# A four-layer graph network on one core: the set-up of its sparse path is laid out anew, in one order for all engines

## The chip, the core and the metric

The kernel runs on one core of a Trainium2 chip. The core has five engines with instruction streams of their own: TensorE (PE in the profile, with its weight loads as PEld), VectorE (DVE), ScalarE (ACT), GpSimd (POOL) and SyncE (SP). SP, ACT and POOL also issue transfers, and an issue stands in the same queue as the engine's other instructions. The metric is the device time of one execution in microseconds (us); lower is better.

## The reference

There are 128 graphs of 64 nodes with 128 features, and one weighted adjacency matrix for each. About a quarter of its entries are not zero, and their values reach just under 6. Four layers follow one another, each `x = layernorm(x + layer(x, adj))`:

```python
# layers 0 and 1: a filter network on every pair (i, j), then a weighted sum over j
f   = exp(coeff * (d_ij - offsets)**2)            # 20 or 64 values for a pair
W   = softplus-like(f @ w1 + b1) @ w2 + b2
agg = einsum('bjf,bijf->bif', y, W * weight_ij)   # layer 0: cosine cutoff at 5; layer 1: adj squared
out = softplus-like(agg @ o1 + c1) @ o2 + c2
# layers 2 and 3: graph convolutions with a normalised adjacency
out = einsum('bij,bjh->bih', norm_A, h @ W) + b
```

The filter network is the bulk of the work. Entries that are zero have a weight of zero in layer 1 and one common filter value in layer 0, so only entries that are not zero need it.

## The kernel before, in words

`sparse_stack` takes two graphs together as a pair (64 pairs, `NP`), eight pairs as a set (`NS` = 8 sets). The nodes of a graph are ranked by how many entries lie below the cutoff (`close`), and the rows of the adjacency are permuted by rank, so that rows of like length can share a fixed number of slots (`CAPS`). For each set `nearest` finds the entries of each row with VectorE's max8 and find-index, and `pack` writes distances (`d`), column numbers (`j`) and weights (`w`) of the slots to DRAM. The main loop has three chunks for each pair and layer (index `i`, `n, k = divmod(i, 3)`): `filter_in` (matmul `px`, exponential), `gather` (matmul `pg` with a one-hot `hot`), `softplus`, `filter_out` (matmul `pw`), `message` (VectorE `m`) and `slot_sums`. At `k` = 0 the loop issues pair n + 2's `d` loads, at `k` = 1 its `j` and `w` loads; `gaussians(n + 1, k)` squares and exponentiates the next pair's `d` on ACT. Searches of later sets run inside the loop, a few steps at a time, from the generator `gathering()`.

Ahead of the loop stands the set-up:

- Four loads of the adjacency (`entries`, L886), two masks on each quarter (L887 and L888), two counts by halving (`count`, L812 to L815). `close` is the difference of these.
- A key for each graph, so that graphs can be sorted by size: `keys`, `place_on`, `to` (L898 to L910). `indirect_dma_start` then scatters the adjacency to `adj_sorted` (2 MB), and later x to `x_sorted` (4 MB, staged in unused parts of `x_all` and `a_all`).
- `rank(0, ...)` (L820 to L842) gives the rank of each node; `rank(1, ...)`, on the degree, is for layer 1.
- `permuted(0)`: set 0 is permuted by matmuls with one-hots (`there`, L1059 and L1060), copied out of PSUM (`rows`), stored to DRAM (`perm`, L1066) and read back in another layout (`ad`, L1071). Later sets are permuted by scatters of POOL, read back at L1052.
- `goes_to(0)` (L980 to L992) makes the places of all pairs in the sorted order, `find_rows` (L997 to L1005) the rows for the output's scatter.
- A small chain gives the filter of a zero entry: `g0`, two activations, `zero_x`, two activations, `zero_w` (L1464 to L1474), and at L1481 VectorE's `zero_filter`.
- `compact(0)` runs `nearest(0)` and `pack(0, 0)`; `loads(0)` and `loads(1)` (L1299) read the slots of the first two pairs, `permuted(1)` and `load_x(1)` (L1331) ready set 1, and two transfers lay out `caps` (L1880, L1881).

The order in an engine's stream is made by a scheduling pass of the framework, unless `in_order` chains instructions to the order in which the program states them:

```python
    before_loop = block[-1]
    in_order(first, before_loop, (nc.vector, nc.gpsimd))
    ...
    in_order(before_loop, block[-1], (nc.tensor, nc.scalar, nc.vector, nc.gpsimd, nc.sync))
```

So in the set-up VectorE and GpSimd are each chained, while the pass is free with PE, ACT and SP, and it may move what stands in the loop ahead of it: in the trace rank 1's pieces lie between those of `nearest(0)`.

Of the kernel before, what the change touches and what calls it, by code (L numbers as in the profile page):

```python
# [12 lines left out]
F32 = mybir.dt.float32  # L13
# [6 lines left out]
P = 128  # L20
# [581 lines left out]
def sparse_stack(ctx: ExitStack, tc: tile.TileContext, t: dict, out: bass.AP, flag):  # L602
# [122 lines left out]

    def load_matrix(name, rows=C):
        w = const.tile([rows, C], F32, name=f"w_{name}")
        nc.scalar.dma_start(w, t[name])
        return w
# [4 lines left out]
    def load_column(name):  # L734
        b = const.tile([P, 1], F32, name=f"c_{name}")
        nc.scalar.dma_start(b, column(name))
        return b
# [19 lines left out]
    def load_rows(name):  # L757
        b = const.tile([P, C], F32, name=f"b_{name}")
        nc.scalar.dma_start(b, dram_ap(t[name], 0, [[0, P], [1, C]]))
        return b  # L760
# [18 lines left out]


# [96 lines left out]
    with (  # L877
        tc.tile_pool(name="count", bufs=2) as pre,
        tc.tile_pool(name="count_ps", bufs=1, space=PSUM) as ps_pre,
    ):  # L880
        entries = pre.tile([NB, A, A], F32, name="entries", bufs=1)
        some = pre.tile([NB, A, A], BF16, name="some", bufs=1)
        within = pre.tile([NB, A, A], BF16, name="within", bufs=1)
        for q in range(4):
            cut = slice(16 * q, 16 * (q + 1))
            nc.sync.dma_start(entries[:, cut, :], adj[:, cut, :])  # L886
            nc.vector.tensor_scalar(within[:, cut, :], entries[:, cut, :], CUTOFF, None, ALU.is_lt)  # L887
            nc.vector.tensor_scalar(some[:, cut, :], entries[:, cut, :], 0.0, None, ALU.is_gt)  # L888

        for into, at in x_parts:  # L890
            nc.sync.dma_start(into, x_flat[:, at])

        degree, close = given[:, 0, :], given[:, 1, :]
        run(deque([count(some, pre, degree), count(within, pre, close)]), -1)
        nc.vector.scalar_tensor_tensor(close, close, -float(A), degree, ALU.add, ALU.add)

        total = const.tile([NB, 1], F32, name="total")
        nc.vector.tensor_reduce(total, given[:, 0:2, :], AX.XY, ALU.add)  # L898
        nc.vector.tensor_scalar(total, total, key_of[:, 0:1], key_of[:, 1:2], ALU.mult, ALU.add)
        keys = pre.tile([P, P], F32, name="keys", bufs=1)  # L900
        nc.vector.tensor_scalar(keys, ident, total, None, ALU.mult)
        keys_ps = ps_pre.tile([P, P], F32, name="keys_ps")
        nc.tensor.matmul(keys_ps, lhsT=all_ones, rhs=keys, start=True, stop=True)
        ranking = deque([rank(0, close, pre)])
        run(ranking, 16)
        nc.vector.tensor_scalar(keys, keys_ps, total, None, ALU.is_gt)
        nc.vector.tensor_reduce(total, keys, AX.X, ALU.add)
        nc.vector.tensor_scalar(place_on, columns, total, None, ALU.is_equal)
        to = const.tile([NB, 1], U32, name="graph_to")
        nc.vector.tensor_copy(to, total)  # L910
        nc.gpsimd.indirect_dma_start(
            out=adj_sorted.rearrange("g i j -> g (i j)"),
            out_offset=bass.IndirectOffsetOnAxis(ap=to, axis=0),
            in_=entries.rearrange("g i j -> g (i j)"), in_offset=None,
        )
        run(ranking, -1)
        nc.vector.tensor_mul(width0, width0, width0)
        nc.vector.reciprocal(coeff0, width0)
        nc.vector.tensor_scalar(coeff0, coeff0, -0.5, None, ALU.mult)
        nc.vector.tensor_scalar(neg_off[0], neg_off[0], -1.0, None, ALU.mult)  # L920

        below = pre.tile([NB, A * A], BF16, name="below", bufs=1)
        nc.scalar.activation(
            below, entries.rearrange("g i j -> g (i j)"), AF.Relu, scale=-1.0, accum_out=odd[:, 0:1]
        )

    work = ctx.enter_context(tc.tile_pool(name="swork", bufs=2))
    node = ctx.enter_context(tc.tile_pool(name="snode", bufs=2))
    ps_x = ctx.enter_context(tc.tile_pool(name="sps_x", bufs=1, space=PSUM))
    ps_g = ctx.enter_context(tc.tile_pool(name="sps_g", bufs=1, space=PSUM))  # L930
    ps_w = ctx.enter_context(tc.tile_pool(name="sps_w", bufs=1, space=PSUM))


    compacting = ctx.enter_context(ExitStack())
    cpt = compacting.enter_context(tc.tile_pool(name="scompact", bufs=1))
# [18 lines left out]


# [15 lines left out]

    def goes_to(i):
        if i == 0:
            sorted_ = ps_n.tile([P, 512], F32, tag="n", name="sorted")[:, 0 : 3 * A]
            nc.tensor.matmul(
                sorted_, lhsT=place_on, rhs=given.rearrange("g k i -> g (k i)"),
                start=True, stop=True,
            )
        from_ = sorted_[:, 2 * A :] if i == 0 else places[1]
        nc.vector.tensor_scalar(codes[i], from_, row[:, 2:3], None, ALU.add)  # L980
        tp = ps_n.tile([P, 512], F32, tag="n", name=f"goes_t{i}")
        nc.tensor.transpose(tp[0:A, 0:P], rows_on if i else codes[0], ident)
        by_pair = tp[0:A, 0:P].rearrange("i (p b) -> i p b", b=2)
        for b in range(2):
            to = slice(b * A, (b + 1) * A)
            nc.vector.tensor_copy(a_all[to, :, A] if i else index[to, :], by_pair[:, :, b])

        code = const.tile([P, A], BF16, name=f"code_b{i}")
        nc.vector.tensor_copy(code, codes[i])
        nc.sync.dma_start(code_dram[i], code)  # L990
        if i == 0:
            nc.vector.tensor_copy(table.rearrange("g k i -> g (k i)"), sorted_[:, 0 : 2 * A])  # L992

    def find_rows():

        tp = ps_n.tile([P, 512], F32, tag="n", name="graphs")
        nc.tensor.matmul(tp[:, 0:P], lhsT=row_wide, rhs=place_on, start=True, stop=True)  # L997
        by_pair = tp[:, 0:P].rearrange("i (p b) -> i p b", b=2)
        row_f = spare[:, 5 * P : 5 * P + NP]
        for b in range(2):  # L1000
            half_ = slice(b * A, (b + 1) * A)
            nc.vector.tensor_scalar(
                row_f[half_], by_pair[half_, :, b], float(A), near[half_], ALU.mult, ALU.add
            )
        nc.vector.tensor_copy(at_row, row_f)  # L1005


# [27 lines left out]
    def permuted(s, again=False):  # L1035
# [18 lines left out]
        if s == 0 and not again:  # L1054
            goes_first()
            flat = ps_x.tile([P, 2, 512], F32, tag="x", name="permuted0")[:, 0, :]
# [11 lines left out]
            )  # L1068
            for h, engine in enumerate((nc.sync, nc.scalar)):
                from_ = perm0.rearrange("k (q h r) j -> h (k q) r j", h=2, r=8)[h]  # L1070
                engine.dma_start(ad[64 * h : 64 * (h + 1), :, 0:A], from_)  # L1071
        permuted_rows[s] = ad
        yield

    def goes_on(s):

# [958 lines left out]
```

## Time and profile before

| | |
|---|---|
| median of 3 runs | 1592.23 us (1591.06 to 1595.87) |
| the profiled execution | 1607.39 us, span 1605.5 us |
| mean granted TensorE clock in it | 0.982 |
| busy in the span | PE 1432.6 us (89%), DVE 1355.6 (84%), ACT 1335.6 (83%), POOL 732.5 (46%) |
| first filter matmul starts | 75.25 us |
| first and fourth message start | 84.89 us and 100.64 us |

A row of the timeline gives the start and the duration in us, the engine, the line of the kernel, the operation, the tile written and those read, how many in a row were merged, and in brackets how long the engine sat idle before it and what ended that. ACTq, SPq and POOLq are issues of transfers; their duration is the issue, not the transfer. A row of waits gives the sum, the times and the longest. A row of a DMA queue gives packets, MB and the share of the 16 engines' time: q0 carries GpSimd's scatters, q1 SP's transfers, q10 ACT's.

### The profile page before, as it was taken

The page shows a single profiled execution, that of the slowest core. Times are in us where ns is not written, and L with a number is a line of the kernel's source. Part 1 is how long each engine was busy: PE and PEld are TensorE (multiplying, and loading weights), DVE is VectorE, ACT ScalarE, POOL GpSimd, SP SyncE. Part 2 cuts the span into 40 slices and gives each one's busy share as a digit, 9 for nine tenths or more (in the row PEclk, how much of TensorE's full clock was granted, in tenths as well). Part 3 has the DMA queues.
Part 4 walks back from the last instruction along what each step waited for, and adds up shares of the span by engine and source line. Part 5 has one row for each costly group of instructions (what it writes and reads, how often), then busy time and mean ns, then how long its engine had stood idle before and what let it go on. Part 6 is the DMA issues. An engine that isn't in the chain of part 4 may idle for free.

```text
span 1605.5 us, 24221 instructions
## 1 busy us (share of the span) xinstructions
PE 1432.6 (89%) x6813; PEld 802.6 (50%) x6813; DVE 1355.6 (84%) x3547; ACT 1335.6 (83%) x1847; POOL 732.5 (46%) x1174
## 2 busy tenths in 40 slices
PE   1276999999999999999999999999999999999974
PEld 1133454555554555555445555556555555555543
DVE  7687889999989999889878888888888888888873
ACT  1266898989888989889999998999989999899842
POOL 2425246555655644425611255433554435543454
PEclk9998999999999999999999999999999999999976
DMA  7654464645455544447555455544554455455200
GB/s 257 209 123 114 112 138 123 135 124 145 124 136 134 136 122 113 113 111 178 149 151 129 128 142 132 129 124 125 144 132 120 120 134 138 124 141 123 64 8 23
DMA packets 122289, 205.67 MB, mean 128 GB/s; under 512 B 47956, under 2 KB 80034, under 8 KB 121506
## 3 DMA queue, kind: packets, MB, share of 16 engines
q1 hardware_dynamic: 110784, 187.61, 46.7%
q0 software_dynamic: 6576, 14.99, 2.9%
q10 hardware_dynamic: 4786, 1.43, 0.4%
q8 instruction: 57, 0.93, 0.3%
q14 instruction: 86, 0.70, 0.2%
HBM read 185.29 MB, written 18.64 MB: 127 GB/s over the span
## 4 chain that ended last, share of the span: by engine, by line
PE 45%; DVE 27%; ACT 10%; DMA 7%; issue 6%; SPq 3%; POOL 2%; another core or an unknown queue 1%; ACTq 0%; DVEq 0%; POOLq 0%
PE pw L1788 16%; PE px L1774 9%; DVE m L1814 8%; PE pg L1800 7%; DVE agg L1837 6%; ACT h L951 4%; DVE hot L1762 2%; DVE at L1182 2%; PE hw L1673 2%; SPq L1299 2%; ACT g L951 2%; PE y L1453 2%; ACT d L951 1%; DVE st L1415 1%; PE o L1584 1%
## 5 line engine op out<-in xcount | busy, mean ns | idle before, releaser
L951 ACT ACTIVATE h<-h,half 128x672 f32<-128x672 f32 (+13 forms) x385 | 353.1, 917 | 0.1
L1837 DVE TENSOR_REDUCE agg<-m 128x16 f32<-128x240 f32 (+13 forms) x896 | 325.0, 411 | 3.0
L951 ACT ACTIVATE g<-pg 128x672 f32<-128x672 f32 (+12 forms) x384 | 303.2, 790 | 26.4 <-DVE m L1814 13.2
L1800 PE MATMUL pg<-hot,ys 64*128 64x336 f32 (+12 forms) x1536 | 308.8, 478 | 7.9 <-DVE hot L1762 7.0
L1788 PE MATMUL pw<-h,w_L_gnn_W2T 128*128 128x420 f32 (+5 forms) x768 | 301.9, 516 | 15.2 <-DVE m L1814 15.2
L1814 DVE SCALAR_TENSOR_TENSOR m<-pw,c_L_gnn_b,g 128x840 f32<-128x840 f32 (+5 forms) x192 | 200.9, 1046 | 115.6 <-PE pw L1788 88.0
L1788 PE MATMUL pw<-h,w_L_gnn_fw 128*128 128x336 f32 (+6 forms) x768 | 264.4, 467 | 28.3 <-DVE m L1814 22.0
L951 ACT ACTIVATE h<-px,c_L_gnn_b 128x840 f32<-128x840 f32 (+5 forms) x192 | 178.7, 931 | 53.6 <-PE px L1774 52.8
L1814 DVE SCALAR_TENSOR_TENSOR m<-pw,c_L_gnn_fb,g 128x672 f32<-128x672 f32 (+6 forms) x192 | 176.9, 921 | 50.0 <-PE pw L1788 31.2
L951 ACT ACTIVATE h<-px,c_L_gnn_fb 128x672 f32<-128x672 f32 (+6 forms) x192 | 159.3, 830 | 71.2 <-PE px L1774 46.4
L1788 PEld LDWEIGHTS pw<-h,w_L_gnn_W2T 128*128 128x128 f32 x768 | 132.5, 191 | 141.1 <-DVE m L1814 37.6
L1774 PE MATMUL px<-d,fw 64*128 64x336 f32 (+6 forms) x768 | 166.2, 507 | 40.8 <-DMA d<-d_dram 29.2
L1800 PEld LDWEIGHTS pg<-hot,ys 64*128 64x128 f32 x1536 | 146.3, 188 | 108.1 <-issue 17.5
L1788 PEld LDWEIGHTS pw<-h,w_L_gnn_fw 128*128 128x128 f32 x768 | 132.5, 191 | 120.6 <-DVE m L1814 62.2
L1762 DVE SCALAR_TENSOR_TENSOR hot<-j,row,w 128x1212 f32<-128x1212 bf16 (+12 forms) x128 | 177.0, 1383 | 9.0 <-issue 9.0
L1774 PE MATMUL px<-d,w1t 64*128 64x420 f32 (+5 forms) x768 | 181.1, 548 | 1.7 <-ACT h L951 1.6
L1422 POOL TENSOR_SCALAR rs<-mv 128x4 f32<-128x4 f32 x61 | 14.5, 237 | 344.0 <-DVE mv L1416 335.6
L1774 PEld LDWEIGHTS px<-d,fw 64*128 64x128 f32 x768 | 59.7, 188 | 132.2 <-ACT h L951 44.4
L951 ACT ACTIVATE d<-d,neg_off 128x1212 f32<-128x1212 f32 (+12 forms) x128 | 119.8, 936 | 7.1 <-issue 7.1
L1428 POOL TENSOR_SCALAR x_all<-ny,mv,rs 128x128 f32<-128x128 f32 x124 | 116.4, 947 | 3.3
L1030 POOL DMA_INDIRECT rows<-comb,goes x64 | 67.9, 1061 | 97.1 <-DMA rows<-comb,goes 69.6
L1774 PEld LDWEIGHTS px<-d,w1t 64*128 64x128 f32 x768 | 57.8, 184 | 66.8 <-ACT g L951 26.8
(264 smaller groups left out, 2209.6 us busy)
## 6 DMA issues: line engine op xcount, KB each, us to landing
d<-d_dram SPq DMA_DIRECT2D x32, 315.0 KB
w<-w_dram SPq DMA_DIRECT2D x32, 315.0 KB
d<-d_dram SPq DMA_DIRECT2D x32, 303.0 KB
w<-w_dram SPq DMA_DIRECT2D x32, 303.0 KB
w<-w_dram SPq DMA_DIRECT2D x32, 252.0 KB
j<-j_dram SPq DMA_DIRECT2D x32, 157.5 KB
j<-j_dram SPq DMA_DIRECT2D x32, 151.5 KB
d<-d_dram SPq DMA_DIRECT2D x16, 300.0 KB
```

Source lines behind the costliest of these rows:

```text
L951: latest = nc.scalar.activation(out_, in_, func, **kw)
L1030: nc.gpsimd.indirect_dma_start(out=into, out_offset=bass.IndirectOffsetOnAxis(ap=at, axis=0), in_=rows, in_offset=None,)
L1182: nc.vector.max_index(out=at[:, r, cut], in_max=top[:, r, cut], in_values=av[:, r, :])
L1299: (engine if name == "d" else nc.sync).dma_start(to, dram_ap(slots[layer, name][s], first, [[0, to.shape[0]], [1, n]]))
L1428: (nc.gpsimd if n == GS else nc.vector).tensor_scalar(dst[:, s, :], y[:, s, :], mv[:, s, 0:1], rstd[:, s : s + 1], ALU.subtract, ALU.mult,)
L1453: nc.tensor.matmul(ps[:, s, :], lhsT=xt[:, s * P : (s + 1) * P], rhs=w["win"], start=True, stop=True)
L1762: nc.vector.scalar_tensor_tensor(hots[n][:, 0:size], j[:, 0:size], near, wt[:, 0:size], ALU.is_equal, ALU.mult)
L1774: nc.tensor.matmul(ps[:, b, 0:n], lhsT=w1, rhs=d[rows, col : col + n], start=True, stop=True)
L1788: nc.tensor.matmul(c["pw"][:, b, :], lhsT=c["w"]["w2"], rhs=c["h"][:, b, :], start=True, stop=True)
L1800: nc.tensor.matmul(ps[:, b, 0:n], lhsT=y[rows, :], rhs=hots[c["n"]][rows, at], start=True, stop=True,)
L1814: nc.vector.scalar_tensor_tensor(messages[n][:, :, at], c["pw"], c["w"]["b2"], c["g"], ALU.add, ALU.mult)
L1837: nc.vector.tensor_reduce(av[:, :, :, r], both, AX.X, ALU.add)
```

## The change

The set-up is stated in a new order, and one chain holds all five engines to it from the start of the set-up to the end of the kernel.

- Layer 0's constants are loaded first, on ACT's queue; those of layer 1 and of the convolutions follow behind the first permutation, on SP's queue.
- The two masks are combined into `within`, so that `close` comes from one count; `rank(0)` follows at once, and `permuted(0)` up to the store of `perm`. The mask `some`, the count `degree`, the graph keys and the scatters of the adjacency and of x stand behind that; the loads of `ad` are stated after the scatters. Set 0's own loads (`load_a(0)` and x) are stated ahead of the loads of the staged x.
- `below` is computed by `act`, which loads ACT's table; the permuted rows use a bank of `ps_n`.
- `goes_to(0)` and two `load_a` follow the later constants; `find_rows` moves to just ahead of the loop. `zero_filter` is stated ahead of the search.
- In `pack(0, 0)` the sine is stated ahead of the store of `j`, the square of `w` is GpSimd's, and the loads of the first two pairs are stated right after the store of `w`. Four of pair 0's six `d` loads are on ACT's queue, the others on SP's.
- `rank(1)` runs to its first halving after those loads and ends after the first one-hot, before the loop; `gathering()` waits 31 steps in its place.

```diff
+    queue = [nc.scalar]            # load_matrix, load_column and load_rows use queue[0]
...
+    layers = [filter_layer(0)]
+    queue[0] = nc.sync
...
+        for cut in quarters:
+            nc.sync.dma_start(entries[:, cut, :], adj[:, cut, :])
+            nc.vector.tensor_scalar(within[:, cut, :], entries[:, cut, :], CUTOFF, None, ALU.is_lt)
+            nc.vector.scalar_tensor_tensor(
+                within[:, cut, :], entries[:, cut, :], 0.0, within[:, cut, :], ALU.is_gt, ALU.mult
+            )
+        load_a(0)
+        nc.sync.dma_start(x_all[:, part(0), :], x_pairs[:, part(0), :])
+        for into, at in x_parts:
+            nc.sync.dma_start(into, x_flat[:, at])
+        below = pre.tile([NB, A * A], BF16, name="below", bufs=1)
+        act(
+            below, entries.rearrange("g i j -> g (i j)"), AF.Relu, scale=-1.0, accum_out=odd[:, 0:1]
+        )
+        degree, close = given[:, 0, :], given[:, 1, :]
+        run(deque([count(within, pre, close), rank(0, close, pre)]), -1)
+        first_rows = permuted(0)
+        next(first_rows)
+        for cut in quarters:
+            nc.vector.tensor_scalar(some[:, cut, :], entries[:, cut, :], 0.0, None, ALU.is_gt)
+        run(deque([count(some, pre, degree)]), -1)
...
+        nc.vector.tensor_copy(to, total)
+        nc.gpsimd.indirect_dma_start(
+            out=adj_sorted.rearrange("g i j -> g (i j)"),
...
+        for into, (from_, _) in zip(x_sorted, x_parts):
+            scatter(into[:, :], from_, to)
+        run(deque([first_rows]), -1)
...
+        if layer + s == 0:
+            sine()
         store("j", jc)
...
-            (nc.gpsimd if s else nc.vector).tensor_tensor(w, w, w, ALU.mult)
+            nc.gpsimd.tensor_tensor(w, w, w, ALU.mult)
...
         store("w", w)
         stored.add((layer, s))
+        if layer + s == 0:
+            slot_data[0] = loads(0)
+            slot_data[1] = loads(1)
+            yield
...
+                    engine = nc.scalar if n == 0 and b * k == 0 else nc.sync
...
-    layers = [filter_layer(0), filter_layer(1)]
+    layers.append(filter_layer(1))
...
-    run(deque([permuted(0)]), -1)
-    goes_to(0)
-    find_rows()
-    for s in (1, 2):
-        load_a(s)
...
+    goes_to(0)
+    for s in (1, 2):
+        load_a(s)
...
-    for into, (from_, _) in zip(x_sorted, x_parts):
-        scatter(into[:, :], from_, to)
-    run(deque([compact(0)]), -1)
     zero_filter = const.tile([P, 1], F32, name="zero_filter")
     nc.vector.tensor_add(zero_filter, u[:, 0:1], w["b2"])
+    first_slots, ranks = compact(0), deque([rank(1, table[:, 0, :], work)])
+    while 0 not in slot_data:
+        next(first_slots)
+    run(ranks, 17)
...
-        yield from rank(1, table[:, 0, :], work)
+        yield from wait_steps(31)
...
-    slot_data[0] = loads(0, nc.scalar)
-    slot_data[1] = loads(1)
     run(deque([permuted(1)]), -1)
     run(deque([load_x(1)]), -1)
...
     one_hot(0)
+    run(ranks, -1)
+    run(deque([first_slots]), -1)
+    find_rows()
...
-    before_loop = block[-1]
-    in_order(first, before_loop, (nc.vector, nc.gpsimd))
...
-    in_order(before_loop, block[-1], (nc.tensor, nc.scalar, nc.vector, nc.gpsimd, nc.sync))
+    in_order(first, block[-1], (nc.tensor, nc.scalar, nc.vector, nc.gpsimd, nc.sync))
```

## The prediction

> **What bounds the kernel now.** First the table of windows (us, then the busy time of PE, its loads, DVE, ACT and POOL), to see which stage the change can reach. In 80 to 100 us TensorE is just getting busy; from about 100 us VectorE is full (26.66 of 27 us), because it compacts later sets beside the messages.
>
> ```profile
> 66.00:80.00 14.00, 3.80 (x12) 1.76 (x12) 2.34 (x6) 4.88 (x7) 9.54 (x10) 1.00 0.67 179
> 80.00:100.00 20.00, 16.03 (x73) 8.21 (x69) 12.63 (x50) 13.50 (x20) 10.38 (x9) 1.00 0.59 139
> 101.00:128.00 27.00, 21.85 (x84) 9.93 (x84) 26.66 (x104) 19.44 (x27) 3.21 (x16) 0.94 0.46 108
> ```
>
> So work after about 100 us takes as long as before, and what the set-up saves is read at the fourth message (100.64 us in the timeline), if every engine and queue is ready for it. Next the timeline of the set-up, for the serial chain: rank (key, code), first permutation (rows, perm, ad), search (same to dc), slot round trip (ACTq d), first filter matmul (px), first message.
>
> ```profile
> 20.71 0.22 DVE L820 SCALAR_TENSOR_TENSOR key<-x_all,order 128x64 f32<-128x64 f32 x1
> 31.82 0.25 DVE L965 TENSOR_SCALAR code<-x_all,row 128x64 f32<-128x64 f32 x1
> 39.30 0.60 ACT L951 ACTIVATE rows<-permuted 128x512 f32<-128x512 f32 x1
> 43.59 0.69 SPq L1071 DMA_DIRECT2D ad<-perm  x1
> 47.39 0.43 DVE L1172 TENSOR_SCALAR same<-ad 128x512 f32<-128x512 f32 x1 [0.20 <-DMA ad<-perm]
> 63.35 0.47 DVE L1097 TENSOR_SCALAR dc<-comb 128x20 f32<-128x20 f32 x4
> 67.58 2.93 ACTq L1299 DMA_DIRECT2D d<-d_dram  x6
> 75.25 1.64 PE L1774 MATMUL px<-d,fw 64*128 64x360 f32 x4 [29.21 <-DMA d<-d_dram]
> 76.64 7.29 SPq L1052 DMA_DIRECT2D ad<-perm  x16
> 83.97 2.76 SPq L1299 DMA_DIRECT2D d<-d_dram  x6
> 90.51 0.59 ACT L951 ACTIVATE d<-d,neg_off 128x360 f32<-128x360 f32 x1
> 100.64 0.97 DVE L1814 SCALAR_TENSOR_TENSOR m<-pw,c_L_gnn_fb,g 128x720 f32<-128x720 f32 x1 [1.23 <-remote]
> ```
>
> SP issues almost without a gap from 63.75 to 114; 83.97 is the load for pair 2, squared at 90.51. Last the waits: ACT's table load, and with it rows, sat behind weight loads; an SP load waited 7.7 us for one it has nothing to do with.
>
> ```profile
> ACT L948 <- DMA w_L_gnn_W<-in_L_gnn_W_dram: 9.6, 1, 9.6
> SPq L1881 <- DMA w_L_gnn_W<-in_L_gnn_W_dram: 7.7, 1, 7.7
> ```
>
> **Part 1, rank first.** The second mask becomes a scalar_tensor_tensor with two inputs; the trace has none of 1024 columns. Bounds 0.66 (the tensor_scalar it follows) and 1.13 (twice the 0.59 step of L1191's 512 columns, less its fixed part); the form is L1191's, so 1.13. Last quarter in at 11.62, as before: 11.62 + 0.61 + 1.13 = 13.4. One count is 3.3 (16.23 to 19.56): 16.7. Rank 0 is 9.6 of VectorE (key 0.26, compares 4.55, count 3.4, bits 1.4): code at 26.3, not 31.8. One-hots to 29.0, matmuls to 31.3 (5.2 after code, less the "sorted" product that stood ahead).
>
> Rows no longer waits for weights, nor for a table of its own (below now loads the one it needs). ACT now has 18 loads, then below (1.28 + 3.8); even if its last load waits for the 3 MB of x (13 us from 8.96 before, 2.5 us more for the two loads put ahead of it), below ends at 30. So rows ends 32.0, against 39.9; perm is written at 32.1 and lands 35.5 (3.4), ad lands 39.3 (3.7). That is 8 us early.
>
> **Part 2, counts behind it.** VectorE after 29.0: four masks 2.65, count 3.3, total and keys 0.9, the PE product to 36.7, is_gt to the graph index 1.05: 37.7 (26.5 before). The sort scatters are issued by POOL from 38.0 (26.87), just after ad lands. Then goes_to(0): product 0.85, code, transpose, copies: 40.2. zero_filter now stands ahead of the search in VectorE's one order, where before it ran at 66.98: it waits for g0, two activations, matmul, two activations, matmul, 2.5 us in the trace (39.80 to 42.32). Search at **43.2**, so 4.2 early; ad is no longer last. The search took 16.43 (47.39 to 63.82), about 0.7 of it rank 1's pieces that did not fall into gaps; they now come later. dc is ready at **T = 59.0**, not 63.8.
>
> **Part 3, the SP queue before T.** From 36.3 SP issues 19 later constants, the code store and two load_a, which need the sorted rows. 6 MB of scatter run meanwhile: adj took 9.4 us from its issue, x 12; one after the other they last from 40.4 to about 57. What small loads get under such a scatter (30 to 36 us before):
>
> ```profile
> q0 software_dynamic: 122, 1.84, 87.0%
> q10 hardware_dynamic: 156, 0.07, 5.9%
> q1 hardware_dynamic: 136, 0.07, 4.3%
> ```
>
> 136 packets in 6 us on SP's queue, against 1989 in the 5.5 us after it. 22 issues at 0.45 would be 10 us, free by 48 with the sorted rows in; the other end is that SP stays behind the scatter and then moves some 1400 packets at about 500 a us: 60. The nearest row, the 7.7 us wait that ended only after the scatter, speaks for the late end: SP ready at **60**, 1.0 behind T. The constants themselves are used late and cost nothing else.
>
> **Part 4, slot round trip.** d, then j stores (1.18 + 1.15): 62.4. w needs table, sine and square: the square moves from VectorE (0.30) to POOL. POOL's own rows:
>
> ```profile
> L1126 POOL TENSOR_TENSOR w<-w x7: 402/1372/1481, 134.9 to 630.7; 128x130 f32<-128x130 f32 x2, 128x141 f32<-128x141 f32 x1, 128x134 f32<-128x134 f32 x1, 128x132 f32<-128x132 f32 x1
> ```
>
> That line is 0.40 alone and 1.37 as a rule. The Trainium skill (GPSIMD Engine Reference, section 1, Specifications) says that GpSimd's SBUF interfaces are shared with VectorE and contended when VectorE has two SBUF inputs; rank 1's compares, just such instructions, are put beside it. By the shortest row w is ready at 61.3 and costs nothing; by the rule at 62.2, still inside the two stores. I take 1.37: w stores end at 63.7.
>
> Pair 0's six d loads go four to ACT, two to SP. The trace has six at 0.49 on ACT, square 3.4 after the last issue. The skill (DMA: Bandwidth & Descriptors, "Issuing engines are not separate DMA queues") speaks against a gain: several issuers save only issue time, usually small beside the transfer. By it, nothing; by the row, two issues, 1.0. I take the row, since issue here is as long as landing; SP's two come after the w stores anyway (64.8). First px at 70.1, 5.1 early: 60, 2.6 from the first store to the first load as in the trace, 0.9 for load_a's small packets ahead of it, issues 2.0, 3.4 to the square, 1.25 for square and exponential.
>
> **Part 5, SP after T.** In the exact order the queue holds, from 60.0: stores to 63.7, d 0.9, j and w 2.1, pair 1's loads 4.8, sixteen ad 7.3, then four x loads (2.4) and the caps pair (0.3 + 1.7 to land + 0.7), which before ran at 55.88, 29.94 and 38.75. Sum 20.2 from 63.7 with 0.6 of gaps: pair 2's d loads at **84.5** to 87.2, landed 90.2. In the trace 83.97: this queue gains nothing. ACT wants the data at 82.0 (15.3 after px in the trace, less the 3.4 of bits and rows_on below) and stalls 8.2. Queued behind the square are the exponential of the fifth chunk, and through it px, pg and pw of the next step: 90.2 + 0.6 + 0.86 + 0.9 + 0.75 + 1.5 = **94.8** for the fourth message. VectorE alone would be there near 92: first message 9.6 after px, then the trace's 15.75 less its 1.2 remote, 1.3 and 1.2 of waits and bits.
>
> Other moves: rank 1's last bits and find_rows now precede the loop on VectorE, 5.4 us between the first one-hot and the first message, inside the 7.4 us that VectorE idles at 84.89; without that cover 5.4 would be on the path. In the loop 1.1 us of bits go (85.78 to 86.96) and a 2.3 us PE wait on rows_on; the SP stall swallows both. POOL's eight permutation scatters wait for load_a, landed about 62, and end before SP reads the last. In-order PE and SP add no other wait that ends last.
>
> **Sum.** 100.64 to 94.8: **5.8 us** less, carried through the full VectorE stage to the end. The profiled execution took 1607.39 (span 1605.5 and 1.9 around it), 15.2 above the median of 1592.23; 10.7 of that is one ACT wait at 147 us labelled remote, out of the change's reach. So I subtract from the median: **1586.4**.
>
> **The rivals.**
> A, SP's round is shorter. Later pairs of ad loads take 0.61 to 0.77 for two (at 119.82 and 189.62), so sixteen could be 5.5, not 7.3; SP ready with T gives 1.0 more. For it: 22 quiet issues are only 10 us. Against: the packet rows, and the sixteen's own row. Fourth message at 92, where VectorE is the limit: 1583.6, and 1581.5 if px lands sooner too.
> B, most of the gain is lost to SP: two to six more us of held issues, for each store and load may wait for an older one as in the 7.7 us row. Pair 2 lands at 92 to 96: 1588.4 to 1592, no change by the 0.3% (4.8 us) that a measurement of this kernel can tell.
> C, slower: the scatters last. Place: SP before the d stores; price: each us that SP is late there moves pair 2's loads one us. Break-even is SP at 66, and a loss of 4.8 needs 71. For it: sharing with 2000 small packets. Against: adj's 2 MB took 9.4 us beside such traffic, which ends all by 61. About 1598.
> D, the reordering does nothing, since the fixed chain of DMA latencies is kept: against it, rows waited 2.3 us after its matmuls and ad ended VectorE's wait; 1592.
>
> **How the numbers follow.** Forecast 0.48, A 0.20, B with D 0.25, C 0.07. Forecast alone: 1584 to 1589 (SP ready 57.6 to 62.6), some three quarters of it over 0.3%. Faster 0.20 + 0.37 + 0.02 of B = 0.59; slower 0.06 of C; the rest, 0.35, is same. The range takes A and B and leaves out C and the ends: 1581 to 1593.5.
>
> **What would show it.** Right: code near 26, rows near 31.4, search near 43, dc near 59, SP's first d store 1 us later, a POOL w of 1.4; pair 2's square the long ACT wait before 91, VectorE idle before the fourth message, that near 95. Wrong: ad landing inside the scatter (search after 45), SP idle before dc, rows behind an ACT load, or a fourth message later than 99.

## The result, and the profile after

The kernel after takes 1587.42 us in the median of 19 runs (1584.36 to 1590.93), the kernel before 1592.88 in as many (1589.88 to 1599.38). The ratio is 0.9956, with a 95% interval of 0.9945 to 0.9966: faster by 7.0 us (5.4 to 8.8) by the ratio, by 5.5 between the medians. The prediction was 1586.4. The profiled execution took 1588.94 us (span 1587.1).

The windows of the kernel after, with the columns of those shown of before:

```profile
66.00:80.00 14.00, 10.71 (x35) 4.96 (x37) 8.23 (x26) 9.22 (x13) 9.02 (x9) 1.00 0.67 160
80.00:100.00 20.00, 14.66 (x52) 6.95 (x48) 14.85 (x58) 10.16 (x15) 10.50 (x10) 0.83 0.63 141
101.00:128.00 27.00, 21.75 (x94) 10.36 (x93) 25.48 (x96) 20.47 (x29) 4.49 (x17) 1.00 0.55 137
```

From 66 to 80 us TensorE now works 10.71 us where it worked 3.80, so the pipeline starts earlier. But from 80 to 100 it does less than before (14.66 against 16.03), and its granted clock falls to 0.83: part of the lead is given back there. The timeline shows how:

```profile
15.75 0.23 DVE L859 SCALAR_TENSOR_TENSOR key<-x_all,order 128x64 f32<-128x64 f32 x1
25.61 0.25 DVE L945 TENSOR_SCALAR code<-x_all,row 128x64 f32<-128x64 f32 x1
30.86 0.60 ACT L933 ACTIVATE rows<-permuted 128x512 f32<-128x512 f32 x1 [1.85 <-PE permuted L1003]
34.13 0.71 SPq L1015 DMA_DIRECT2D ad<-perm  x1
42.69 0.16 DVE L1495 TENSOR_TENSOR zero_filter<-zero_w,c_L_gnn_fb 128x1 f32<-128x1 f32 x1 [2.61 <-PE zero_w L1491]
42.92 0.40 DVE L1228 TENSOR_SCALAR same<-ad 128x512 f32<-128x512 f32 x1
58.25 1.01 SPq L1022 DMA_DIRECT2D a_all<-adj_sorted  x2
59.36 1.49 SPq L1157 DMA_DIRECT2D d_dram<-dc  x2
60.62 0.98 POOL L1178 TENSOR_TENSOR w<-w 128x139 f32<-128x139 f32 x1 [2.05 <-ACT w L933]
67.74 1.64 PE L1792 MATMUL px<-d,fw 64*128 64x360 f32 x4 [18.59 <-ACT d L933]
71.10 1.34 DVE L1780 SCALAR_TENSOR_TENSOR hot<-j,row,w 128x1080 f32<-128x1080 bf16 x1 [6.02 <-DMA d<-d_dram]
72.75 7.68 SPq L995 DMA_DIRECT2D ad<-perm  x16
77.56 1.48 PE L1806 MATMUL pw<-h,w_L_gnn_fw 128*128 128x360 f32 x4
80.24 0.97 DVE L1832 SCALAR_TENSOR_TENSOR m<-pw,c_L_gnn_fb,g 128x720 f32<-128x720 f32 x1
80.48 1.80 SPq L1385 DMA_DIRECT2D x_all<-x_sorted  x4
82.33 0.29 SPq L1896 DMA_DIRECT2D caps_dram<-caps_row  x1
85.36 0.69 SPq L1897 DMA_DIRECT2D caps<-caps_dram  x1
86.10 2.33 SPq L1354 DMA_DIRECT2D d<-d_dram  x6
89.96 0.59 ACT L933 ACTIVATE d<-d,neg_off 128x360 f32<-128x360 f32 x1 [7.11 <-DMA d<-d_dram]
96.93 0.97 DVE L1832 SCALAR_TENSOR_TENSOR m<-pw,c_L_gnn_fb,g 128x720 f32<-128x720 f32 x1 [3.60 <-PE pw L1806]
```

Read it as a row of leads over before. `code` is 6.2 us earlier, `rows` 8.4, the search (`same`) 4.5, because it now waits for `zero_filter` and no longer for `ad`. The first `px` is 7.5 earlier (67.74 against 75.25), but the first message only 4.7 (80.24 against 84.89). Its one-hot (`hot`) starts 3.4 us after `px`, where it was 0.9 before, and from there VectorE works without a gap on the end of rank 1, two pieces of the search and `find_rows`; it comes to the message 1.2 us after `pw` has ended (79.04). The third message is 6.1 earlier (88.15 against 94.23). Meanwhile SP's queue is busy through the ad, x and caps rows, and the six `d` loads of pair 2 start 2.1 us later than they did (86.10 against 83.97). ScalarE stands 7.11 us for them, and the fourth message is only 3.7 us earlier (96.93 against 100.64).

### The profile page after: what moved, and what is told of

Same layout as the page of the kernel before. It is cut to its first block, busy times and chain, and to the rows that moved or that the text cites. A ratio compares the mean times of both kernels' runs of the same rounds, so it can differ in the third digit from the quotient of the medians.

```text
span 1587.1 us, 24220 instructions
## 1 busy us (share of the span) xinstructions
PE 1432.6 (90%) x6806; PEld 804.1 (51%) x6813; DVE 1362.3 (86%) x3549; ACT 1334.0 (84%) x1846; POOL 731.4 (46%) x1175
## 4 chain that ended last, share of the span: by engine, by line
PE 45%; DVE 28%; ACT 10%; DMA 6%; issue 5%; SPq 4%; POOL 1%; DVEq 0%; ACTq 0%; POOLq 0%
PE pw L1806 16%; PE px L1792 9%; DVE m L1832 7%; PE pg L1818 7%; DVE agg L1855 5%; ACT h L933 5%; DVE hot L1780 3%; SPq L1354 2%; DMA w<-w_dram 2%; PE hw L1691 2%; ACT g L933 2%; DVE st L1428 2%; PE y L1466 2%; ACT d L933 1%; DVE at L1238 1%
## 5 line engine op out<-in xcount | busy, mean ns | idle before, releaser
L1792 PEld LDWEIGHTS px<-d,w1t 64*128 64x128 f32 x768 | 57.8, 184 | 66.8 <-ACT g L933 25.7
```

The source lines that it names most:

```text
L1792: nc.tensor.matmul(ps[:, b, 0:n], lhsT=w1, rhs=d[rows, col : col + n], start=True, stop=True)
```

## The experiments

Three theories were tested. **S**: the round of SP's queue decides, that is, when pair 2's `d` loads land. **V**: the serial chain decides, up to the start of the search and the first `px`. **N**: what the set-up saves is lost or won at stalls further on, by chance. Rival C of the prediction (the scatters last and hold the first `d` store) was tested too. The table gives the places that tell them apart, in us of each profile, and the ratio to the kernel before with its interval; 0.001 is 1.6 us.

| kernel | search | first d store | first px | fourth message | ratio |
|---|---|---|---|---|---|
| before | 47.39 | 65.00 | 75.25 | 100.64 | 1 |
| before, again | 47.66 | 65.27 | 73.91 | 98.65 | 1 |
| after | 42.92 | 59.36 | 67.74 | 96.93 | 0.9956 [0.9945, 0.9966] |
| after, again | 42.94 | 59.39 | 68.12 | 96.96 | 0.9949 [0.9933, 0.9966] |
| x, caps late | 42.63 | 58.83 | 67.17 | 92.39 | 0.9935 [0.9919, 0.9951] |
| zero_filter late | 40.16 | 59.27 | 67.56 | 94.98 | 0.9956 [0.9940, 0.9971] |
| constants late | 42.73 | 58.64 | 66.77 | 95.47 | 0.9951 [0.9935, 0.9966] |
| one chain on before | 51.67 | 69.07 | 78.17 | 109.67 | 1.0042 [1.0028, 1.0055] |
| no chain on after | 44.82 | 60.73 | 68.95 | 95.20 | 0.9956 [0.9940, 0.9971] |
| those three late | 39.92 | 56.79 | 64.89 | 90.14 | 0.9926 [0.9904, 0.9947] |
| degree ahead of rank | 57.49 | 73.44 | 81.60 | 110.69 | 1.0051 [1.0032, 1.0069] |
| the same, scatters wait | 43.74 | 64.81 | 73.01 | 101.05 | 0.9996 [0.9986, 1.0006] |
| all d loads on ScalarE | 42.74 | 59.17 | 70.76 | 96.04 | 0.9968 [0.9959, 0.9977] |
| search ahead of places | 37.60 | 54.44 | 64.46 | 88.65 | 0.9922 [0.9902, 0.9941] |

The fourth message is a fair meter of large steps: from the last row to "degree ahead of rank" it moves 22.0 us, and the time 0.0129, or 20.5 us. Single rows stray from the straight line between these two by up to 3.5 us (the kernel after, again, is 3.5 faster than it, and the second profile of before 3.1 slower), so smaller steps are read from the profile and not from the time.

The chips differ. "One chain on before", "no chain on after", "those three late" and "degree ahead of rank" ran on a chip where the kernel before took 1609.63 us (29 runs); for each kernel the ratio compares runs on one chip.

### The kernel after, again

> The changed kernel once more, for a second profile. Theory S (SP's queue sets the loop's start: pair 2's d loads wait behind SP's round of some 45 issues): the set-up repeats, ACT waits 6.5 to 7.5 us for pair 2's square, the fourth message starts at 96.5 to 97.5 us; ratio to before 0.995 to 0.997. Theory N (what goes beyond the 3.7 us at the fourth message comes from stalls by chance in the loop): the shift of the last message against a second profile of the kernel before is 3.7 plus or minus 1.5, and the ratio drifts to 0.9975.

1586.92 us. The set-up repeats within 0.4 us at every place of the table, and the fourth message within 0.03. ScalarE's wait for pair 2's square is 7.70, a little above the range given. The drift to 0.9975 that N expected did not come.

### x and caps late

```diff
-    run(deque([load_x(1)]), -1)
-    nc.sync.dma_start(caps_dram, caps_row...)
-    nc.sync.dma_start(caps..., dram_ap(caps_dram, ...))
...
+        if i == 5:      # in the loop
+            run(deque([load_x(1)]), -1)
+            nc.sync.dma_start(caps_dram, caps_row...)
+        if i == 8:
+            nc.sync.dma_start(caps..., dram_ap(caps_dram, ...))
```

> After, but load_x(1) and the caps store are issued at loop step 5, the caps load at step 8, so that SP has six issues (5.6 us from 80.48 to 86.10) less before pair 2's d loads. S: these loads start at 80.5, ACT's wait for the square falls from 7.1 to under 2 us, VectorE's 3.6 us of idle time before the fourth message goes, the message starts near 93; 3.5 to 4.5 us faster than after, 1583 to 1584. Theory V (the serial chain up to the first filter matmul is what counts, SP is hidden): that chain is untouched, so no change, within 1 us of after.

SP's `d` loads for pair 2, ScalarE's square of them and the fourth message, in this kernel's timeline:

```profile
79.56 2.18 SPq L1354 DMA_DIRECT2D d<-d_dram  x6
83.28 0.59 ACT L933 ACTIVATE d<-d,neg_off 128x360 f32<-128x360 f32 x1 [1.28 <-DMA d<-d_dram]
92.39 0.96 DVE L1832 SCALAR_TENSOR_TENSOR m<-pw,c_L_gnn_fb,g 128x720 f32<-128x720 f32 x1
```

The six loads stand 6.5 us earlier than in the kernel after, ScalarE's stall falls from 7.11 to 1.28, and VectorE no longer idles before the fourth message. First `px` moved by 0.6, the message by 4.5: that is S and not V. The time fell by 2.1 between medians taken on one chip, less than the 3.5 to 4.5 expected, and the intervals of the two ratios overlap: the places show S, the time alone does not.

### zero_filter late

```diff
-    zero_filter = const.tile([P, 1], F32, name="zero_filter")
-    nc.vector.tensor_add(zero_filter, u[:, 0:1], w["b2"])
     first_slots, ranks = compact(0), ...
     while 0 not in slot_data:
         next(first_slots)
+    zero_filter = ...
```

> After, but VectorE's zero_filter is stated behind the search, so that VectorE no longer waits 2.6 us for zero_w; the search starts near 40.2 us and dc is ready at 56.1. V: everything behind it comes 2.6 us earlier, 1584.8. S: SP issues constants and load_a until 59.3, so the first d store stays at 59.3, and the change is under 0.5 us.

The search starts 2.8 us earlier and the slots are ready 1.8 earlier, but the first `d` store stays at 59.27, behind the constants and `load_a` on SP. First `px` and the time do not move. What does move is told by the windows in steps of 2 us (PE, loads, DVE, ACT, POOL, then the clock) and by the matmuls of the fourth step. First both of the kernel after:

```profile
92.00:94.00 2.00, 2.00 (x8) 0.68 (x4) 1.30 (x3) 2.00 (x4) 1.28 (x1) 0.50 0.79 216
94.00:96.00 2.00, 2.00 (x5) 1.18 (x4) 0.00 (x0) 1.91 (x3) 0.00 (x0) 0.50 1.24 217
```

```profile
91.35 1.57 PE L1792 MATMUL px<-d,fw 64*128 64x360 f32 x4 [3.31 <-ACT h L933]
94.06 2.77 PE L1806 MATMUL pw<-h,w_L_gnn_fw 128*128 128x360 f32 x4
```

Then both of this kernel, and its earlier rows from 86 to 88 us:

```profile
86.00:88.00 2.00, 2.00 (x11) 1.94 (x10) 0.93 (x8) 0.00 (x0) 1.70 (x2) 0.50 0.40 102
92.00:94.00 2.00, 1.99 (x8) 0.69 (x6) 2.00 (x17) 2.00 (x4) 0.00 (x0) 1.00 0.98 239
```

```profile
87.92 1.85 PE L1806 MATMUL pw<-h,w_L_gnn_fw 128*128 128x360 f32 x4
91.05 0.88 PE L1792 MATMUL px<-d,fw 64*128 64x360 f32 x4 [1.27 <-ACT h L933]
92.52 1.48 PE L1806 MATMUL pw<-h,w_L_gnn_fw 128*128 128x360 f32 x4
```

In the kernel after TensorE idled 3.31 us in ScalarE's stall, and its granted clock was 0.50 from 91.0 to 97.8 us: `px` took 1.57 in place of 0.88, `pw` 2.77 in place of 1.48. Here the clock was 1.00 at that place, and the fourth message came 2.0 us earlier, with ScalarE's square at nearly the same time (89.66 against 89.96). But the clock fell here too, only earlier: it was 0.50 from 85.5 to 88.9, while ScalarE was standing still anyway, so the slow `pw` at 87.92 cost nothing, and it was full again when the data came. Nothing in the edit aims at that, so these 2.0 us are luck, as far as the traces show. The Trainium skill (TensorE: Matmul & The Clock Gate, Part 1: The HAM clock gate) says that the clock is halved after an idle window of about 3.4 us. The 3.31 us are near that, but TensorE had idled only 1.70 us just before the fall in this kernel, and 2.7 to 2.8 us in three kernels below; the measurement decides, and the length of one idle time does not tell by itself when the clock falls. A stall upstream can thus cost its length and then a slow stage. That the time did not follow the 2.0 us says little for N, since they lie within its interval (0.0015 to either side, or 2.4 us).

### Constants late

```diff
-    layers.append(filter_layer(1))
-    g["W0"], g["W1"], g["W2"] = ...
+        if i == 20:     # in the loop, on SP
+            layers.append(filter_layer(1))
+            g["W0"], g["W1"], g["W2"] = ...
```

> After, but the 19 constants of layer 1 and of the convolutions are loaded at loop step 20 instead of ahead of the search. S: SP is idle before dc, stores d at once (58.9 instead of 59.4), load_a lands earlier and no longer stands ahead of the stores in the queue: first px 1 us earlier, pair 2's loads 0.5 us earlier, 0.5 to 1 us faster. V: the first px comes 1 us earlier and all with it: 1 us. Rival C (the constants under the scatters are what costs): SP free 5 us or more sooner than dc, and over 2 us faster.

SP is free for `load_a` at 45.12, not 58.25, so the first `d` store follows its data: 58.64, 0.7 earlier. The fourth message comes 1.5 earlier, and the time is the same. The trace shows where the 1.5 us went: the constants, moved into the loop, hold SP from 151.16 to 161.96, the next `d` loads wait behind them, ScalarE stands for these, and the 25th message and those that follow are 1.0 us later than in the kernel after.

```profile
168.94 0.60 ACT L933 ACTIVATE d<-d,neg_off 128x364 f32<-128x364 f32 x1 [4.44 <-DMA d<-d_dram]
```

So the time does not say what the constants cost where they stood; the first store does. In the kernel after, constants and scatters together hold the first store by under a microsecond: rival C falls.

### One chain on before, and no chain on after

```diff
 # one chain on before
-    before_loop = block[-1]
-    in_order(first, before_loop, (nc.vector, nc.gpsimd))
...
-    in_order(before_loop, block[-1], (nc.tensor, nc.scalar, nc.vector, nc.gpsimd, nc.sync))
+    in_order(first, block[-1], (nc.tensor, nc.scalar, nc.vector, nc.gpsimd, nc.sync))
```

> The kernel before, with one edit: a single chain over all five engines from the start of the set-up, as in the change, and nothing stated anew. So the order as the old program states it is held on TensorE, ScalarE and SP too: rank 1, which the pass had moved between the pieces of the first search, falls back into the loop; all constants stand ahead of the rows on ScalarE; the loads of x and caps fall behind the first slots' loads on SP. If the chain itself brought the gain, this is 1585 to 1588. By S (SP's round) x and caps now cost pair 2's loads about 4 to 6 us as they do in the kernel after, without its earlier start: first px near 75, fourth message 102 to 105, 1594 to 1600. By V (the serial chain up to the first px counts) no change: 1592 to 1594.

```profile
40.54 3.65 PE L1060 MATMUL permuted<-a_all,there 128*128 128x64 f32 x16 [10.85 <-DMA a_all<-in_adj_dram]
44.23 0.60 ACT L951 ACTIVATE rows<-permuted 128x512 f32<-128x512 f32 x1 [7.30 <-PE permuted L1060]
```

Slower by 6.7 us (0.0042 of 1592.5). Held to the old program, set 0's own adjacency (`load_a(0)`) is loaded behind the staged x, and the permutation's matmuls wait for it until 40.54; x and caps also move between pair 1's and pair 2's loads. `code` itself was earlier than before (28.97 against 31.82). The chain is no gain by itself. The converse, the diff above turned round on the kernel after:

> The kernel after with the chains of before: in the set-up VectorE and GpSimd alone are held, and the pass is free with TensorE, ScalarE and SP. The pass then puts the 19 later constants ahead of the store of perm on SP, the caps pair ahead of the loads of ad, two of the four x loads ahead of the d store, and the loads of the first filter weights last on ScalarE. By S, pair 2's d loads come 3 to 5 us sooner than 85.4 after the first px (the caps pair and two x loads no longer stand between): fourth message 92 to 94, 1584 to 1586, unless perm waits behind the constants. By V what counts is the start of the search and first px: perm up to 2 us late, px 68 to 70, 1587 to 1589. If one order for all engines is what brings the gain, 1590 or more.

0.9956, as with the chain. The pass puts the caps pair and two x loads ahead of the first store, so pair 2's loads stand at 81.72, as expected; but the search starts 1.9 later, and the fourth message is at 95.2, not at 92 to 94. With the new order stated, the chain is worth nothing that can be measured here (the interval is 2.4 us to either side).

### Degree ahead of rank

```diff
         degree, close = given[:, 0, :], given[:, 1, :]
+        for cut in quarters:
+            nc.vector.tensor_scalar(some[:, cut, :], entries[:, cut, :], 0.0, None, ALU.is_gt)
+        run(deque([count(some, pre, degree)]), -1)
         run(deque([count(within, pre, close), rank(0, close, pre)]), -1)
         first_rows = permuted(0)
         next(first_rows)
-        for cut in quarters: ...
-        run(deque([count(some, pre, degree)]), -1)
```

> The kernel after with rank first undone: the four masks some and the count of the degree (5.7 us of VectorE, 28.38 to 34.3 in the profile) stand ahead of the count and rank of close, as before; all else stays. VectorE's sum up to the search is the same, the scatters are still issued near 37.5; only the permutation's transfers lose the cover of those 5.7 us. code at 31.3, rows near 36.5, ad lands near 42.5. The search waits for zero_filter until 42.9 in the kernel after, so by S and by this sum it starts at 43 to 44, the d store stays at 59.3 to 60, and the time is that of the kernel after: 1586.5 to 1588. If rank first is what brings the gain (code 5.7 us earlier, carried to px), it is 1590 to 1592.

Both expected numbers were wrong: 1.0051, or 8.1 us slower than before and some 15 slower than after. The timeline, and the DMA queues from 48 to 52 us (packets, MB, share of the 16 engines):

```profile
38.46 1.21 POOL L1073 DMA_INDIRECT adj_sorted<-entries,graph_to  x1 [30.14 <-DVE graph_to L1072]
39.82 0.71 SPq L1015 DMA_DIRECT2D ad<-perm  x1
57.49 0.43 DVE L1228 TENSOR_SCALAR same<-ad 128x512 f32<-128x512 f32 x1 [13.56 <-DMA ad<-perm]
```

```profile
q0 software_dynamic: 65, 1.60, 92.6%
q10 hardware_dynamic: 64, 0.02, 1.8%
q1 hardware_dynamic: 64, 0.02, 1.8%
```

`ad` was issued 1.4 us behind the scatter, and the search that waits for it starts 17.7 us after that issue. In the kernel after it is issued 3.4 us ahead of the scatter, and the search never waits for it; in the kernel "search ahead of places" below, where the search does, it takes 3.7 us. Under the scatter SP's and ScalarE's queues moved 64 packets each in 4 us, against 65 of the scatter, which are of 25 KB in the mean. The Trainium skill (DMA: Bandwidth & Descriptors, Queues, rings and completion order) says that a DMA engine takes its queues in turn, one whole packet from each. The equal counts agree with that: a queue of small packets gets a turn as often, and almost none of the bytes.

### The same, with the scatters held until ad has landed

```diff
         nc.vector.tensor_copy(to, total)
+        run(deque([first_rows]), -1)
+        nc.gpsimd.tensor_copy(keys[:, 0:1], permuted_rows[0][:, 0, 0:1])
         nc.gpsimd.indirect_dma_start(
...
-        run(deque([first_rows]), -1)
```

> The kernel with the degree ahead of rank again, where ad's loads were issued at 39.82, 1.4 us behind the issue of the graph scatter, and landed only at 57.5. Here GpSimd copies one column of ad ahead of the three scatters, so they are issued only when ad has landed; nothing else differs. If ad was starved by the scatters, it lands 3.4 us after its issue as in the kernel after: search at 43.5 (57.49 without the copy), scatters issued at 43.8 to 46.6 in place of 38.5 to 41.2. They then end near 63.5 (20 us after the first issue, as in the kernel after), SP, which holds load_a ahead of the slots, is free near 65, first px at 73 to 74 (near 82 without the copy), fourth message 102 to 103 (110.69), 0.998 to 1.000 of the kernel before. If it was something else that held ad (its own rows, the late rank), the search stays at 55 to 58 and the time at 1.005.

```profile
39.73 0.71 SPq L1015 DMA_DIRECT2D ad<-perm  x1
43.56 0.18 POOL L1074 COPY keys<-ad 128x1 f32<-128x1 f32 x1 [35.23 <-DMA ad<-perm]
43.74 0.39 DVE L1229 TENSOR_SCALAR same<-ad 128x512 f32<-128x512 f32 x1
44.51 1.52 POOL L1075 DMA_INDIRECT adj_sorted<-entries,graph_to  x1 [0.76 <-DMA neg_off<-in_neg_offsets_dram]
```

The starvation is gone: search at 43.74 in place of 57.49, and 0.9996, the time of the kernel before. The search starts almost as in the kernel after, and yet 6.4 us of the time (0.9996 less 0.9956) are lost: the scatters are issued 7.0 us later, and behind them `load_a` and the first `d` store (64.81 against 59.36). So without rank first none of the gain is left, whether `ad` falls behind the scatters or the scatters wait for it. With rank first the permutation passes ahead of the scatters, and they need not wait. That the other parts of the change are worth nothing does not follow; most of them were not undone one by one.

### All of pair 0's d loads on ScalarE's queue

```diff
-                    engine = nc.scalar if n == 0 and b * k == 0 else nc.sync
+                    engine = nc.scalar if n == 0 else nc.sync
```

> The kernel after with all six of pair 0's first d loads on ScalarE's queue, as before: the two of SP are issued by ScalarE behind its four. By S SP saves two issues (0.9 us) ahead of pair 1's loads, so pair 2's d loads come up to 0.9 sooner (84.5 for 85.4), while first px comes 0.7 to 1.0 later (68.8 to 69.1 for 68.12): fourth message 96 to 97, time that of the kernel after within 1 us. By V it is 1 us slower: 1587.5 to 1588.5. By the rule that several issuers save nothing when the transfer is the longer part, px stays at 68.1.

First `px` is 2.6 us later (70.76), so neither the 0.7 to 1.0 us came nor the 68.1 of the rule that part 4 of the prediction cites; pair 2's loads stand at 85.78, not clearly sooner (86.10 and 85.40 in the two profiles of the kernel after).

```profile
80.93 0.97 DVE L1832 SCALAR_TENSOR_TENSOR m<-pw,c_L_gnn_fb,g 128x720 f32<-128x720 f32 x1 [1.23 <-PE goes_t L1099]
```

Of the 2.6 us some 1 is left at the first message (80.93 against 80.24 and 79.75), since in the kernel after VectorE was busy with other work until then, and nothing at pair 2's square (89.98 against 89.96). The fourth message is at 96.04, 0.9 earlier: `px` still ran at full clock after 2.73 us of idle time, and the clock fell to 0.50 only at 92.5. The ratio is 0.0012 to 0.0019 higher than those of the kernel after, or 2 to 3 us, with intervals that overlap. So the second queue is worth 2.6 us at the first matmul and nothing that this profile shows at the fourth message; why the time is higher, if it is, stays open.

### Those three late, and the search ahead of the places

```diff
 # those three late: the three diffs above together; and on top of it, search ahead of places:
-    goes_to(0)
     for s in (1, 2):
         load_a(s)
...
     nc.vector.tensor_add(zero_filter, u[:, 0:1], w["b2"])
+    goes_to(0)
     run(ranks, 17)
```

> Three earlier edits on the kernel after together: the x loads and the caps store moved into the loop at step 5, the caps load at step 8; zero_filter behind the search; the 19 later constants in the loop from step 20. Alone, each of the last two freed one end of the d store and left the other (ready data 56.9 but the store at 59.3; an empty queue but data at 58.8). Together the d store goes at 56.4 to 57.2, first px at 64.5 to 65.5, pair 2's d loads at 76.5 to 77.5, and ScalarE has no long wait for them. By S the fourth message is at 89.5 to 90.5 (2 to 3 us before the 92.39 of late x and caps alone), and by the rate that edit showed (4.6 us at the fourth message, 2.1 in the time) 1582 to 1584. By V 1584.5 to 1585 (2.3 us from px alone). By N (what is saved in the set-up is lost at stalls further on) no different from late x and caps alone: 1584.8.

The store at 56.79, `px` at 64.89 and the fourth message at 90.14 are where S put them. 0.9926 is 11.8 us faster than before, some 4.8 faster than after by the ratios; on the 1592.5 of the other chips it is 1580.7, a little under the 1582 to 1584 expected.

> The best so far (late x, caps, zero_filter and constants) with goes_to(0), 2.7 us of VectorE between 37.2 and 39.9, moved behind the first slots. The search starts at 37.3 to 37.6 (39.92), data ready at 53.9 to 54.3 (56.72), px 62 to 62.5 if nothing else holds. The graph and x scatters end at 55 to 56, so the first d store now falls under them: if they starve its 2 transfers and the loads behind them, px is at 63.5 to 64.9, no gain. Fourth message 87.5 to 88.5 in the first case, 89.5 to 90 in the second; 0.9905 to 0.992 and 0.9925 of the kernel before.

```profile
37.60 0.43 DVE L1228 TENSOR_SCALAR same<-ad 128x512 f32<-128x512 f32 x1 [0.39 <-DMA ad<-perm]
54.44 1.21 SPq L1157 DMA_DIRECT2D d_dram<-dc  x2
63.19 0.59 ACT L933 ACTIVATE d<-d,neg_off 128x360 f32<-128x360 f32 x1 [1.10 <-DMA d<-d_dram]
64.46 1.64 PE L1787 MATMUL px<-d,fw 64*128 64x360 f32 x4 [7.96 <-DMA j<-j_dram]
```

The search starts 2.3 us earlier, and the store too; but from the store to the square it now takes 8.75 us where it took 6.8 (56.79 to 63.61), which fits a store that falls under the end of the scatters (0.13 MB of them still moved between 54.4 and 56.5). `px` gains 0.4, the fourth message 1.5, and the time (0.9922, 1580.77 us) cannot be told from the last one. This is the fastest version; its interval (0.9902 to 0.9941) lies below that of the kernel after in its 19 runs.

### The kernel before, again

> The kernel before once more, to see which of its stalls repeat. The set-up should (search near 47.4, first px near 75.25, fourth message near 100.6). If the 10.7 us wait of ScalarE at 147 us is in the program, it is there again, and the profile of the kernel after, where it is missing, gained it by the change; if it is chance, it is gone or elsewhere, and the two messages stand apart by 3.7 us from the fourth on.

ScalarE's long wait in the first profile of before, and the waits over 5 us in the profile of "degree ahead of rank":

```profile
158.09 0.86 ACT L951 ACTIVATE h<-px,c_L_gnn_fb 128x720 f32<-128x720 f32 x1 [10.68 <-remote]
```

```profile
162.73 0.60 ACT L933 ACTIVATE zt<-zT 128x512 f32<-128x512 f32 x1 [5.58 <-remote]
168.50 0.86 ACT L933 ACTIVATE h<-px,c_L_gnn_fb 128x720 f32<-128x720 f32 x1 [5.17 <-remote]
```

In the second profile of before it is missing. Messages slip by 13 to 15 us at that place in the first profile of before and in all four kernels of the chip that was slower by 17 us, with old and new set-up alike, and in no other profile. So it belongs to the chip or the execution, and the prediction was right to leave it out. The set-up did not repeat in full: first `px` came 1.3 us earlier (73.91), since the square of pair 0 followed the last of ScalarE's six issues by 1.9 us and not by 3.4. The fourth message was 2.0 us earlier than in the first profile, without the 1.23 us remote wait.

## Why the prediction was right, and where its steps were not

**Ahead of the search** (parts 1 and 2) the sums held: `code` 25.61 for 26.3, `rows` done at 31.5 for 32.0, search at 42.92 for 43.2, and it waits for `zero_filter`, not `ad`. What the prediction did not say is why the 8 us of the permutation count although the search starts only 4.5 earlier: they keep `ad` clear of the scatters. It saw that the scatters follow "just after ad lands", and named "ad landing inside the scatter" among the signs of being wrong; the experiment shows it as the chief hazard of this set-up.

**SP ahead of the first store** (part 3): ready at 59.36 for 60, behind constants that were starved as the packet rows said. Its data (`dc`) were complete at 58.75, so the queue cost 0.6 us, and the later experiment puts it at 0.7, against the 1.0 taken.

**Slot round trip** (part 4): the w square took 0.98, for 1.37, and costs nothing either way; what VectorE beside it had in that is not shown by any run. `px` came at 67.74, 2.4 earlier than 70.1. The term that was too large is that of the loads' landing. The first load came 3.75 us after the store (63.11), for 3.5; from there to the square the working has 5.4 (2.0 of issues and 3.4 from the last issue, as in the trace of before), and the trace of after 3.35 (66.46). The 3.4 was read from one profile; the second profile of before has 1.9. The first message did not keep that gain: 80.24, where 9.6 us after the forecast `px` is 79.7. It came 12.5 us after `px`: the one-hot started 2.5 us later after it than before, and the work put ahead of the message on VectorE took 7.9 us (72.36 to 80.24), 1.2 beyond the end of `pw`, where 5.4 were to lie inside idle time.

**SP after the store** (part 5): the mechanism was right, and it is what decided. Pair 2's loads stood at 86.10 for 84.5, though the first store had gone 0.6 earlier than forecast. Two terms were undersized: pair 1's loads held the queue 5.8 us (66.91 to 72.75) for 4.8, and the load of caps followed its store by 3.0 us, for 2.0 (0.3 + 1.7); the x loads took 1.8 for 2.4. ScalarE stalled 7.11 for 8.2, and the square stood at 89.96, near the 90.2 at which the data were to land. The next term failed: from there to the fourth message 4.6 us were summed with matmuls at full clock, and it took 7.0, since TensorE ran at half clock after its idle time. Hence 96.93 for 94.8.

**Sum.** The message was forecast 5.8 us earlier and came 3.7 earlier (1.7 against the second profile of before), while the runs gave 5.5 to 7.0. So the size was met closer than its steps were, and that is in part luck. The profiled executions take 1607.39 and 1590.03 before, the first with 12.9 us of the remote wait, and 1588.94 and 1587.87 after: without that wait 1592.3 and 1588.4 in the mean, 3.9 apart. The second of before was a quick one; 5 of the 43 runs on its chip beat it. Of the other 1.5 to 3 us the traces place a part at the far end of the kernel. In both profiles of before TensorE's clock was 0.50 for 3.4 us there, and the 382nd and 383rd of the 384 messages start 6.0 and 5.7 us apart; in both of after the clock falls only behind the last message, and it is 4.4. From the last message to the end it takes 64.9 and 65.6 us before, 66.8 and 65.2 after, so not all of that is kept. "Constants late" has the slow stage too (5.9), and five other variants do not (4.4). So it hangs on where idle time falls, which is what N says; two profiles of a kernel do not tell how often.

**The rivals.** A and C fell: SP's sixteen ad loads took 7.68, no less than the 7.3 taken, and the scatters end in time. B has a share, since pair 2's loads came 2.1 us later than before where 0.5 was taken. C is out in this kernel, but its mechanism is there where the scatters start 7 us later: with the scatters held, the first store stands at 64.81, 5 us behind its data. D is refuted by the result and by the pair of experiments on rank first.

## What to carry to other kernels

Ask of each small transfer on the serial chain which bulk transfer will be in flight when it is issued: an order that puts it a few microseconds ahead of the bulk can be worth more than the work that it saves. Then follow the queue that issues the loads past the first result, for the second and third items may wait where the first no longer does; moving transfers that nobody needs yet out of that round was, at the fourth message, the larger part of what could still be gained here (4.5 of 8.3 us). A chain that fixes an order is worth what the stated order is worth, and made the old one slower.

## What the runs showed of the hardware

- Two queues of small packets and one of large ones moved 64, 64 and 65 packets in the same 4 us; the large one had all but 3% of the bytes. From the issue of `ad`, 256 KB in all, to the search it took 17.7 us in place of 3.7.
- After 3.31 us without work TensorE's granted clock was 0.50 for 6.8 us, and a matmul group of 1.48 us took 2.77. In other kernels it fell with shorter idle times just before (1.70 in "zero_filter late", 2.73 in "all d loads on ScalarE", 2.69 in "degree ahead of rank"), and stayed 0.50 for 3.4 us or 6.8.
- The store and the load of a small table through DRAM (caps) stood 2.3 to 3.1 us apart on SP in seven profiles, with nothing else issued between them.
- Four kernels on one chip, and the first profile of before, whose chip is not known, lost 13 to 15 us at one place, where the traces label waits remote; the nine other profiles lost nothing there.
